# The opening of layer 0: vector order by hand, one loading queue, row weights through DRAM, three early pieces between first scores

## Chip, core and metric

The kernel runs on one core of one Trainium2 chip. The metric is device time in microseconds (us), the median of the runs shown. A separate profiled execution of the kernel gives the durations used for reasoning.

## The reference, cut to what matters

Four layers of attention and feed-forward run one after another on x of 4 batches (blocks) of 256 tokens by 256. The change lies in the attention of layer 0, which reads a context ctx of 1601 rows per block, and touches two later users of the context:

```python
# layer 0: attention of every token to its block's context
h = layernorm(x)                                   # 4 x 256 x 256
s = einsum('bsd,bmd->bsm', h, ctx) / 16            # 4 x 256 x 1601
s = where(mask[:, None, :], s, -1e30)
out = einsum('bsm,bmd->bsd', softmax(s), ctx)
x = x + where(any(mask, -1)[:, None, None], out, 0)
```

Layer 1 needs a weighted sum of the context rows. The weight of a row is a running sum of powers of sigmoid(decay), and a sum of these weights is needed too. Layer 2 needs keys and values of the context, products of ctx with weights, which depend on nothing that layers 0 and 1 compute.

## The kernel before, in words

Everything is fp32. Each program line is handed to a scheduler, which may reorder independent instructions of an engine; `pin` (line 99) holds an instruction behind the one that was written before it on the same engine. Each engine then works through its own list in order, and so do the queues on which SP and ACT issue DMAs.

`setup` (line 140) issues the loads of the four token blocks on SP's queue (L152) and lets POOL make the identity and constants.

`l0_xattn` (line 165) loads, for each block, the transposed context (ctxT; block 0 in four pieces, L183, the others whole, L136) and the plain context (ctxn, L188), on SP's queue. Two buffers hold ctxn, so the third load waits for a free one. Then it creates the generator of the early pieces (L190), which loads its weights (L1203, L1207). `hidden` (L192) brings a block's mask to all partitions by ACT's queue and turns it into an additive mask in two POOL steps. A second small mask load, and VectorE's muf, anym and anyd (L207 to L211), give for each block whether any row is valid; a product with ones spreads this to anyb. The row weights are a sigmoid on ACT (L216), a scan on one partition (L220) and a sum (L224). `spread_weights` (L230) copies them to all partitions by five products with a row of ones (L236) and five ACT copies (L238).

The main loop runs over 4 blocks and two halves q of 128 tokens. `turned` (L241) normalizes a block (statistics, root on ACT, reciprocal, scaling), turns it by four TensorE transposes (L248) and copies it (L250). `scores` (L253) makes the score products of one half (16 matmul instructions of up to 512 columns), adds the mask with a running maximum on VectorE (L260, two instructions), and takes the exponential on ACT (L268). Its PSUM tile has one buffer of four banks, so the next scores wait for this exponential. `values` (L274) turns the probabilities in groups of four (L284), evicts them alternately by VectorE and ACT (L71, L73) and multiplies with ctxn; the result goes into x (L297). The values of one half are written after the scores of the next. Last in each turn stands the weighted context sum csum for layer 1 (L314, eight in all), which needs ctxT and the spread weights.

An early piece (`l2_early`, line 1194) is either a product piece of layer 2's keys and values (8 matmul instructions, two ACT evictions, one store of va) or a turn piece (four transposes, one eviction, one store). There are 165: per unit seven product pieces, then four turns of the unit before. `fill(n)` (line 109) takes the next n of them. Fixed numbers are taken at fixed places: in `l0_ffn` 34 (F0, line 46), in `l0_add` 81 (G0), later 48, and the last two are taken in layer 2's attention, where the softmax of its first unit is prepared. Before the change none is taken in `l0_xattn`.

Of the kernel before, what the change touches and what calls it, by code (L numbers as in the profile page):

```python
# [11 lines left out]
F32 = mybir.dt.float32  # L12
BF16 = mybir.dt.bfloat16
U8 = mybir.dt.uint8
# [18 lines left out]
NEG = -1e30  # L33
# [7 lines left out]
NH2, NKV2, HD2 = 16, 4, 128  # L41
# [17 lines left out]
class Kernel:  # L59
    def __init__(self, ctx, tc, ins, out):  # L60
        self.ctx, self.tc, self.nc = ctx, tc, tc.nc
        self.i, self.out = ins, out
        self.flip = 0
        self.flip4 = False


# [73 lines left out]
    def setup(self):  # L140
        nc, tc, ctx, i = self.nc, self.tc, self.ctx, self.i
        const = self.const = ctx.enter_context(tc.tile_pool(name="const", bufs=1))
        self.small = ctx.enter_context(tc.tile_pool(name="small", bufs=3))
        xp = ctx.enter_context(tc.tile_pool(name="x", bufs=1))
        self.xn = ctx.enter_context(tc.tile_pool(name="xn", bufs=2))
        self.xnT = ctx.enter_context(tc.tile_pool(name="xnT", bufs=2))
        self.dram = ctx.enter_context(tc.tile_pool(name="dram", bufs=2, space=DRAM))

        self.x = []
        for b in range(B):  # L150
            t = xp.tile([P, 2, D], F32, name=f"x{b}")
            nc.sync.dma_start(t, i["x"][b].rearrange("(q p) d -> p q d", p=P))  # L152
            self.x.append(t)

        self.ident = const.tile([P, P], F32, name="ident")
        make_identity(nc, self.ident)
        self.ones = const.tile([P, P], F32, name="ones")
        nc.gpsimd.memset(self.ones, 1.0)
        self.eps5 = const.tile([P, 1], F32, name="eps5")
        nc.gpsimd.memset(self.eps5, 1e-5)  # L160
        self.eps6 = const.tile([P, 1], F32, name="eps6")
        nc.gpsimd.memset(self.eps6, 1e-6)


    def l0_xattn(self):
        nc, tc, i = self.nc, self.tc, self.i
        with ExitStack() as es:
            one = es.enter_context(tc.tile_pool(name="a0one", bufs=1))
            two = es.enter_context(tc.tile_pool(name="a0", bufs=2))
            ps_s = es.enter_context(tc.tile_pool(name="a0s", bufs=1, space=PSUM))  # L170
            ps = es.enter_context(tc.tile_pool(name="a0p", bufs=2, space=PSUM))
# [4 lines left out]
            ctxn, ctxT = [], []  # L176
            for b in range(B):
                pool = self.e2 if b < 2 else one
                if b == 0:
                    t = pool.tile([P, 2, MP], F32, name="ctxT", bufs=2)  # L180
                    v = i["ctxT"][b].rearrange("(k p) m -> p k m", p=P)
                    for c0 in range(0, MP, 512):
                        nc.sync.dma_start(t[:, :, c0 : min(MP, c0 + 512)], v[:, :, c0 : min(MP, c0 + 512)])  # L183
                else:
                    t = self.load_ctxT(pool, b, 2)
                ctxT.append(t)
                t = two.tile([P, NM, D], F32, name="ctxn")
                nc.sync.dma_start(t, i["ctx"][b].rearrange("(m p) d -> p m d", p=P))  # L188
                ctxn.append(t)
            self.early = self.l2_early(ctxT)  # L190

            def hidden(b):  # L192


                mu = two.tile([P, M], U8, name="mub")
                nc.scalar.dma_start(mu, i["mask"][b : b + 1].to_broadcast([P, M]))
                mf = two.tile([P, M], F32, name="mfb")
                nc.gpsimd.tensor_copy(mf, mu)
                nc.gpsimd.tensor_scalar(mf, mf, -NEG * 16.0, NEG * 16.0, ALU.mult, ALU.add)
                return mf  # L200
# [5 lines left out]
            muf = one.tile([B, M], F32, name="muf", tag="row")  # L206
            nc.vector.tensor_copy(muf, mu)  # L207
            anym = one.tile([B, 1], F32, name="anym")
            nc.vector.tensor_reduce(anym, muf, AX.X, ALU.max)
            anyd = one.tile([B, B], F32, name="anyd")  # L210
            nc.vector.tensor_scalar(anyd, self.ident[:B, :B], anym, None, ALU.mult)  # L211


            dec = one.tile([1, 1], F32, name="dec")
            nc.scalar.dma_start(dec, i["decay"])
            nc.scalar.activation(dec, dec, AF.Sigmoid)  # L216
            orow = one.tile([1, M], F32, name="orow", tag="row")
            nc.gpsimd.memset(orow, 1.0)
            wrow = one.tile([1, M], F32, name="wrow")
            nc.vector.tensor_tensor_scan(  # L220
                wrow[:, ::-1], dec.to_broadcast([1, M]), orow, 0.0, ALU.mult, ALU.add
            )
            sw = one.tile([1, 1], F32, name="sw")
            nc.vector.tensor_reduce(sw, wrow, AX.X, ALU.add)  # L224
            misc = ps1.tile([P, 512], F32, name="misc1", tag="misc")
            self.mm(misc[:, 0:B], self.ones[:B, :], anyd, True, True)
            anyb = one.tile([P, B], F32, name="anyb")
            nc.vector.tensor_copy(anyb, misc[:, 0:B])

            def spread_weights():  # L230
                w = one.tile([P, M], F32, name="wall")
                for c0, c1 in (*CC, (M, M + 1)):
                    t = ps1.tile([P, 512], F32, name="misc2", tag="misc")
                    row, to = (sw, self.swb) if c0 == M else (wrow[:, c0:c1], w[:, c0:c1])
                    tc.keep_in_program_order(
                        nc.tensor.matmul(t[:, : c1 - c0], self.ones[:1, :], row, start=True, stop=True)  # L236
                    )
                    nc.scalar.copy(to, t[:, : c1 - c0])  # L238
                return w
# [13 lines left out]
            def scores(b, q, xT):  # L253
                s = ps_s.tile([P, 2048], F32, name="s0")
                for c0, c1 in CC:
                    for k in range(2):
                        self.mm(s[:, c0:c1], xT[:, k, q * P : (q + 1) * P], ctxT[b][:, k, c0:c1], k == 0, k == 1)
# [10 lines left out]
                nc.scalar.activation(p, s[:, :M], AF.Exp, bias=nm, scale=1.0 / 16.0, accum_out=sm)  # L268
# [30 lines left out]
            last = wall = None  # L299
            xT = turned(0)  # L300
            for b in range(B):
                for q in range(2):
                    now = (b, q, *scores(b, q, xT))
                    if q == 1 and b + 1 < B:
                        xT = turned(b + 1)
                    if q == 0 and b + 1 < B:
                        mask.append(hidden(b + 1))
                    if last is not None:
                        values(*last)
                    if wall is None:  # L310
                        wall = spread_weights()

                    junk = one.tile([P, M], F32, name="junk0", tag="row")
                    nc.vector.tensor_tensor_reduce(  # L314
                        junk, ctxT[b][:, q, :M], wall, 1.0, 0.0, ALU.mult, ALU.add, self.csum[:, q, b : b + 1]
                    )
                    last = now
            values(*last)

# [874 lines left out]
    def l2_early(self, ctxT):  # L1194
# [9 lines left out]
        w = []  # L1204
# [7 lines left out]
        def products(u):  # L1212
# [3 lines left out]
            for m in range(0, NM, 2):  # L1216
# [3 lines left out]
                for t in range(n):  # L1220
                    for k in range(2):
                        c0 = (m + t) * P
                        self.mm(tp[:rows, t, :], ctxT[u // NKV2][:, k, c0 : c0 + rows], w[u % NKV2][:, k, :], k == 0, k == 1)
# [1016 lines left out]
```

## Time and profile before

| what | value |
|---|---|
| median of 3 runs | 2660.19 us (2654.16 to 2660.89) |
| the profiled execution's own time | 2609.97 us |
| its span, first to last instruction | 2608.2 us |
| mean granted TensorE clock | 0.979 |
| TensorE busy (matmuls) | 2472.6 us, 95% |
| VectorE, ScalarE (ACT), GpSimd (POOL) busy | 57%, 50%, 29% |
| first score product starts | 16.27 us |
| fourth scores (block 1, second half) start | 64.79 us |

A share is an average over the whole span; what a step of the opening costs has to be read from that stretch. In timeline lines the columns are start, duration (both us), engine, line, operation, output and inputs, count, and in brackets how long the engine stood idle before it and what ended that. The profiled execution is about 50 us shorter than the runs of the median, so differences within it are carried over, not its level.

### The profile page before, as it was taken

To read this page: it belongs to the slowest core of one execution; us is meant where nothing else is said; L and a number is where in the kernel's file an instruction comes from. 1 tells how busy PE (TensorE), PEld (TensorE's weight loads), DVE (VectorE), ACT (ScalarE), POOL (GpSimd) and SP (SyncE) were. 2 spreads that over 40 slices of the span, in tenths; PEclk is the share of its full clock that TensorE was granted. 3 is DMA by queue.
4 is the path that set the end of the run, shared out by engine and by line. 5 is a ranking of instruction groups with operands and counts; after the bars stand their busy time and mean duration, and the time that the engine had idled before them with its cause. 6 is when DMAs were issued, how large, how long until landed. Compare 5 with 4: busy or idle time off the path is not lost. (4 is left out here: it accounts for less than half of the span.)

```text
span 2608.2 us, 47024 instructions
## 1 busy us (share of the span) xinstructions
PE 2472.6 (95%) x17800; PEld 1512.2 (58%) x17816; DVE 1473.9 (57%) x3039; ACT 1307.1 (50%) x2955; POOL 751.9 (29%) x1030
## 2 busy tenths in 40 slices
PE   7989978999899999999999999998998999999997
PEld 4678967777455555555555555655564544545553
DVE  6344537635677777777777777673334314334323
ACT  2335545424544445444544454532326766857775
POOL 1015646132444334334334444332102001011000
PEclk8999999899999999999999999998999999999998
DMA  5155686626311111111111110004211100000000
GB/s 203 61 190 164 187 174 206 202 67 211 114 47 39 47 47 47 47 42 36 46 46 39 47 47 21 9 1 165 99 60 55 34 1 28 4 4 2 6 6 5
DMA packets 94654, 186.24 MB, mean 71 GB/s; under 512 B 15052, under 2 KB 62864, under 8 KB 93232
## 3 DMA queue, kind: packets, MB, share of 16 engines
q1 hardware_dynamic: 78278, 144.90, 16.4%
q0 software_dynamic: 10416, 28.46, 4.9%
q10 hardware_dynamic: 5738, 9.87, 1.2%
q8 instruction: 145, 2.38, 0.4%
q14 instruction: 77, 0.63, 0.1%
HBM read 136.77 MB, written 46.42 MB: 70 GB/s over the span
## 5 line engine op out<-in xcount | busy, mean ns | idle before, releaser
L1496 ACT ACTIVATE p<-s,nm 128x448 f32<-128x448 f32 (+1 forms) x512 | 326.9, 645 | 423.4 <-DVE nm L1492 259.1
L1957 ACT ACTIVATE e<-s 128x1024 f32<-128x1024 f32 (+1 forms) x448 | 404.3, 960 | 158.2 <-PE s L76 153.1
L76 PE MATMUL s<-kT,qT 128*32 128x448 f32 (+1 forms) x4096 | 470.2, 556 | 10.0 <-ACT p L1496 5.0
L76 PE MATMUL o<-pT,va 128*128 128x256 f32 (+2 forms) x1920 | 431.0, 376 | 6.1 <-DVE pT L1538 6.1
L1532 POOL TENSOR_SCALAR p<-p,rm 128x448 f32<-128x448 f32 (+1 forms) x512 | 323.3, 659 | 369.5 <-DVE rm L1525 339.2
L76 PEld LDWEIGHTS o<-pT,va 128*128 128x128 f32 (+1 forms) x1920 | 344.4, 191 | 93.0 <-issue 51.5
L1538 DVE STREAM_TRANSPOSE pT<-p 128x896 f32<-128x896 f32 (+1 forms) x256 | 283.8, 1127 | 37.2 <-POOL p L1532 33.5
L1492 DVE TENSOR_REDUCE nm<-s 128x2 f32<-128x896 f32 (+1 forms) x256 | 282.6, 1104 | 3.3
L76 PE MATMUL s<-qb,kT 32*128 32x256 f32 (+1 forms) x3328 | 267.6, 404 | 13.2 <-ACT e L1957 11.0
L76 PEld LDWEIGHTS s<-kT,qT 128*32 128x32 f32 x4096 | 123.6, 109 | 265.0 <-issue 223.4
L76 PE MATMUL o<-e,va 128*32 128x256 f32 (+1 forms) x3328 | 235.7, 391 | 1.2 <-DVE os L2054 1.2
L76 PEld LDWEIGHTS s<-qb,kT 32*128 32x128 f32 (+1 forms) x3328 | 162.9, 181 | 105.0 <-issue 75.4
L76 PEld LDWEIGHTS o<-e,va 128*32 128x32 f32 (+1 forms) x3328 | 90.5, 110 | 115.0 <-issue 74.9
L1984 POOL TENSOR_TENSOR x<-x,t 128x32 f32<-128x32 f32 x64 | 14.7, 252 | 438.4 <-DVE t L1979 438.4
L76 PE MATMUL fill<-wkc_early,ctxT 128*128 128x256 f32 (+1 forms) x532 | 130.7, 394 | 8.2 <-ACT kT_early L1252 7.8
L1489 DVE TENSOR_TENSOR s<-s,mask 128x128 f32<-128x128 f32 (+1 forms) x256 | 83.0, 325 | 67.5 <-PE s L76 62.8
L76 PEld LDWEIGHTS fill<-wkc_early,ctxT 128*128 128x128 f32 (+1 forms) x532 | 102.0, 196 | 26.2 <-ACT kT_early L1252 10.3
L431 POOL DMA_INDIRECT f0xr<-f0xd,f0src x95 | 92.0, 968 | 50.8 <-PE f0tph L488 42.3
L1384 POOL TENSOR_TENSOR qo<-qo,qt 128x512 f32<-128x512 f32 x32 | 41.1, 1284 | 225.2 <-DVE rm L1525 139.7
L1496 ACT ACTIVATION_READ_ACCUMULATOR p<-s,nm 128x1 f32 x512 | 101.7, 199 | 0.0
L76 PE MATMUL f2gu<-f2wgu,f2xsT 128*128 x176 | 85.6, 611 | 0.6 <-issue 0.3
L529 POOL DMA_INDIRECT f0yt<-f0yd,f0slot x64 | 66.8, 1044 | 47.5 <-DMA vd<-va_early 16.3
(517 smaller groups left out, 3567.4 us busy)
## 6 DMA issues: line engine op xcount, KB each, us to landing
ctxT<-in_ctxT SPq DMA_DIRECT2D x10, 1664.0 KB, 10.6
f0yd<-f0ys SPq DMA_DIRECT2D x95, 128.0 KB, 2.8
vd<-va_early SPq DMA_DIRECT2D x90, 128.0 KB, 2.5
kd<-kT_early SPq DMA_DIRECT2D x45, 256.0 KB, 2.5
kT<-kd SPq DMA_DIRECT2D x15, 768.0 KB, 4.2
va<-vd SPq DMA_DIRECT2D x15, 768.0 KB, 6.0
wq<-in_l_wq SPq DMA_DIRECT2D x16, 512.0 KB, 3.3
wo<-in_l_wo SPq DMA_DIRECT2D x16, 512.0 KB, 3.1
```

The lines of the kernel that those rows point to most:

```text
L76: self.nc.tensor.matmul(out, lhsT, rhs, start=start, stop=stop, **kw)
L431: nc.gpsimd.indirect_dma_start(out=t, out_offset=None, in_=xd[:, :], in_offset=bass.IndirectOffsetOnAxis(ap=src[:, n : n + 1], axis=0),)
L529: nc.gpsimd.indirect_dma_start(out=yt, out_offset=None, in_=yd[:, :], in_offset=bass.IndirectOffsetOnAxis(ap=slot[:, t, r : r + 1], axis=0),)
L1384: nc.gpsimd.tensor_tensor(o1, o1, t2, ALU.add)
L1489: nc.vector.tensor_tensor(sv, sv, mask[:, 2 * c : 2 * c + 2, : nt - CT, :].rearrange("p n t i -> p n (t i)"), ALU.add)
L1492: nc.vector.tensor_reduce(nm[:, 2 * c : 2 * c + 2], s[:, :, : nt * 32], AX.X, ALU.max, negate=True)
L1496: nc.scalar.activation(p[:, n, : nt * 32], s[:, n, : nt * 32], AF.Exp, bias=nm[:, e : e + 1], accum_out=sm[:, e : e + 1],)
L1532: nc.gpsimd.tensor_scalar(p[:, n, : nt * 32], p[:, n, : nt * 32], r[:, e : e + 1], 1.0, ALU.mult, ALU.mult)
L1538: nc.vector.transpose(pT[:, 2 * c : 2 * c + 2, :nt, :].rearrange("p n t i -> p n (t i)"), p[:, :, : nt * 32])
L1957: nc.scalar.activation(e[:kr, :, :n, :], s[t][:kr, :, :n, :], AF.Exp, scale=1.0 / math.sqrt(HD3))
L1984: nc.gpsimd.tensor_tensor(xt, xt, t[:, q], ALU.add)
```

## The change

- SP's queue gets the loads in the order: tokens of block 0, mask of block 0, ctxT of block 0, tokens of blocks 1 to 3, the early pieces' weights, then the other context loads as before. The masks of blocks 1 to 3 stay on ACT's queue, pinned.
- VectorE's work of the opening is pinned: the statistics and scaling of block 0, then the statistics of blocks 1 to 3, from which one root and one reciprocal serve three blocks. A dummy root loads ACT's table first; ten transposes of the identity with no use run on TensorE.
- The small mask load and muf, anym, anyd, anyb go. Whether any row is valid is read from the running maximum in the instruction that scales the result.
- The sigmoid becomes an exponential on ACT and an addition and reciprocal on VectorE. The scan follows the first mask addition; its sum is an accumulating ACT copy. The row goes to DRAM and comes back to all partitions by two DMAs on ACT's queue, in place of the five products and copies.
- The weighted sums of block 0 move into the first turn of block 1 (three in that turn), all pinned.
- After the first scores three early pieces are taken, their matmuls pinned on TensorE, as are the scores of block 0. `take` gives them tiles of the `tp` tag, which gets three buffers instead of two.

The diff, cut to its core:

```diff
-            nc.sync.dma_start(t, i["x"][b].rearrange("(q p) d -> p q d", p=P))
+        nc.scalar.activation(const.tile([P, 1], F32, name="root"), self.eps5, AF.Sqrt)
...
+            token(0)
+            nc.scalar.dma_start(dec, i["decay"])
+            hidden(0, nc.sync)
...
+                if b == 0:
+                    for n in range(1, B):
+                        token(n)
+                    self.early = self.l2_early(ctxT)
...
-            mu = one.tile([B, M], U8, name="mu")
-            nc.scalar.dma_start(mu, i["mask"])
-            mask = [hidden(0)]
-            nc.vector.tensor_copy(muf, mu)
-            nc.vector.tensor_reduce(anym, muf, AX.X, ALU.max)
-            nc.vector.tensor_scalar(anyd, self.ident[:B, :B], anym, None, ALU.mult)
-            nc.scalar.activation(dec, dec, AF.Sigmoid)
...
+            def weights():
+                self.pin(nc.vector.tensor_scalar(dec, dec, 1.0, None, ALU.add))
+                self.pin(nc.vector.reciprocal(dec, dec))
+                wrow = one.tile([1, M + 1], F32, name="wrow")
+                self.pin(nc.vector.tensor_tensor_scan(
+                    wrow[:, :M][:, ::-1], dec.to_broadcast([1, M]), self.ones[:1, :1].to_broadcast([1, M]), 0.0,
+                    ALU.mult, ALU.add,
+                ))
+                self.pin(nc.scalar.activation(junk, wrow[:, :M], AF.Copy, accum_out=wrow[:, M:]))
+                wd = self.dram.tile([1, M + 1], F32, name="wrowd")
+                nc.scalar.dma_start(wd, wrow)
+                nc.scalar.dma_start(wall, wd[:, :M].to_broadcast([P, M]))
+                nc.scalar.dma_start(self.swb, wd[:, M:].to_broadcast([P, 1]))
...
-                self.layernorm(xn, self.x[b])
+                for q in range(2):
+                    self.pin(nc.vector.tensor_scalar(
+                        xn[:, q, :], self.x[b][:, q, :], mv[:, b, q, 0:1], rs[:, b, q : q + 1], ALU.subtract, ALU.mult
+                    ))
...
+                        if b == 0:
+                            self.pin(ins)
...
+                if b + q == 0:
+                    weights()
...
-                nc.vector.tensor_tensor(r, r, anyb[:, b : b + 1], ALU.mult)
+                nc.vector.scalar_tensor_tensor(r, mx[:, 1:2], NEG * 8.0, r, ALU.is_gt, ALU.mult)
...
+            for n in range(10):
+                nc.tensor.transpose(t[:, :P], self.ident, self.ident)
...
+            for b0, b1 in ((0, 1), (1, B)):
+                for b in range(b0, b1):
+                    for q in range(2):
+                        st = self.small.tile([P, 6], F32, name="st0")
+                        self.pin(nc.vector.bn_stats(st, self.x[b][:, q, :]))
+                        self.pin(nc.vector.bn_aggr(mv[:, b, q, :], st))
+                self.rstd(rs[:, b0:b1], mv[:, b0:b1, :, 1], 1.0, self.eps5)
+                if b0 == 0:
+                    xT = turned(0)
+            self.pin(nc.scalar.activation(dec, dec, AF.Exp, scale=-1.0))
...
                     now = (b, q, *scores(b, q, xT))
+                    if last is None:
+                        self.hold = True
+                        self.fill(3)
+                        self.hold = False
...
+                    for c in [] if b == 0 else [(0, 0), (0, 1), (1, 0)] if (b, q) == (1, 0) else [(b, q)]:
+                        self.pin(nc.vector.tensor_tensor_reduce(
+                            junk, ctxT[c[0]][:, c[1], :M], wall, 1.0, 0.0, ALU.mult, ALU.add,
+                            self.csum[:, c[1], c[0] : c[0] + 1],
+                        ))
```

More of the change, by code (lines that the diff above doesn't have):

```diff
@@ L150, in setup @@
         for b in range(B):
[L151 to L153 removed]
+            self.x.append(xp.tile([P, 2, D], F32, name=f"x{b}"))
         self.ident = const.tile([P, P], F32, name="ident")
@@ L170, in l0_xattn, with token, hidden @@
             ps_s = es.enter_context(tc.tile_pool(name="a0s", bufs=1, space=PSUM))
-            ps = es.enter_context(tc.tile_pool(name="a0p", bufs=2, space=PSUM))
+            ps = es.enter_context(tc.tile_pool(name="a0p", bufs=3, space=PSUM))
             ps1 = es.enter_context(tc.tile_pool(name="a0q", bufs=1, space=PSUM))
             CC = [(c, min(M, c + 512)) for c in range(0, M, 512)]
-            ctxn, ctxT = [], []
+            ctxn, ctxT, mask = [], [], []
+            def token(b):
+                nc.sync.dma_start(self.x[b], i["x"][b].rearrange("(q p) d -> p q d", p=P))
+            def hidden(b, eng):
+                mu = two.tile([P, M], U8, name="mub")
+                ins = eng.dma_start(mu, i["mask"][b : b + 1].to_broadcast([P, M]))
+                if b:
+                    self.pin(ins)
+                mf = two.tile([P, M], F32, name="mfb")
+                nc.gpsimd.tensor_copy(mf, mu)
+                nc.gpsimd.tensor_scalar(mf, mf, -NEG * 16.0, NEG * 16.0, ALU.mult, ALU.add)
+                mask.append(mf)
+            dec = one.tile([1, 1], F32, name="dec")
+            token(0)
+            nc.scalar.dma_start(dec, i["decay"])
+            hidden(0, nc.sync)
             for b in range(B):
@@ L189, in l0_xattn @@
                 ctxn.append(t)
[L190 to L200, printed above, removed]
-            mu = one.tile([B, M], U8, name="mu")
@@ L204, in l0_xattn @@
-            nc.scalar.dma_start(mu, i["mask"])
-            mask = [hidden(0)]
-            muf = one.tile([B, M], F32, name="muf", tag="row")
-            nc.vector.tensor_copy(muf, mu)
-            anym = one.tile([B, 1], F32, name="anym")
-            nc.vector.tensor_reduce(anym, muf, AX.X, ALU.max)
[L210 to L215, printed above, removed]
@@ L216, in l0_xattn @@
-            nc.scalar.activation(dec, dec, AF.Sigmoid)
[L217 to L239, printed above, removed]
+            self.take = lambda: ps.tile([P, 512], F32, name="fill0", tag="tp")
@@ new lines, in l0_xattn @@
+            wall = one.tile([P, M], F32, name="wall")
+            def weights():
[6 more added lines that the diff above has]
+                ))
+                junk = one.tile([1, M], F32, name="junkw", tag="row")
+                self.pin(nc.scalar.activation(junk, wrow[:, :M], AF.Copy, accum_out=wrow[:, M:]))
[3 more added lines that the diff above has]
+                nc.scalar.dma_start(self.swb, wd[:, M:].to_broadcast([P, 1]))
@@ L256, in scores @@
                     for k in range(2):
-                        self.mm(s[:, c0:c1], xT[:, k, q * P : (q + 1) * P], ctxT[b][:, k, c0:c1], k == 0, k == 1)
+                        ins = nc.tensor.matmul(
+                            s[:, c0:c1], xT[:, k, q * P : (q + 1) * P], ctxT[b][:, k, c0:c1], start=k == 0, stop=k == 1
+                        )
+                        if b == 0:
+                            self.pin(ins)
                 mx = self.small.tile([P, 2], F32, name="mx0")
@@ L297, in values @@
                 nc.vector.scalar_tensor_tensor(xt, av, r, xt, ALU.mult, ALU.add)
-            last = wall = None
-            xT = turned(0)
+            t = ps.tile([P, 512], F32, name="idle", tag="tp")
+            for n in range(10):
+                nc.tensor.transpose(t[:, :P], self.ident, self.ident)
+            mv = one.tile([P, B, 2, 2], F32, name="mv0")
+            rs = one.tile([P, B, 2], F32, name="rs0")
+            for b0, b1 in ((0, 1), (1, B)):
[8 more added lines that the diff above has]
+            self.pin(nc.scalar.activation(dec, dec, AF.Exp, scale=-1.0))
+            last = None
             for b in range(B):
@@ L303, in l0_xattn @@
                     now = (b, q, *scores(b, q, xT))
+                    if last is None:
+                        self.hold = True
+                        self.fill(3)
+                        self.hold = False
                     if q == 1 and b + 1 < B:
@@ L306, in l0_xattn @@
                     if q == 0 and b + 1 < B:
-                        mask.append(hidden(b + 1))
+                        hidden(b + 1, nc.scalar)
                     if last is not None:
                         values(*last)
[L310 to L316, printed above, removed]
+                    for c in [] if b == 0 else [(0, 0), (0, 1), (1, 0)] if (b, q) == (1, 0) else [(b, q)]:
+                        junk = one.tile([P, M], F32, name="junk0", tag="row")
+                        self.pin(nc.vector.tensor_tensor_reduce(
+                            junk, ctxT[c[0]][:, c[1], :M], wall, 1.0, 0.0, ALU.mult, ALU.add,
+                            self.csum[:, c[1], c[0] : c[0] + 1],
+                        ))
                     last = now
@@ L1222, in products @@
                         c0 = (m + t) * P
-                        self.mm(tp[:rows, t, :], ctxT[u // NKV2][:, k, c0 : c0 + rows], w[u % NKV2][:, k, :], k == 0, k == 1)
+                        ins = nc.tensor.matmul(
+                            tp[:rows, t, :], ctxT[u // NKV2][:, k, c0 : c0 + rows], w[u % NKV2][:, k, :],
+                            start=k == 0, stop=k == 1,
+                        )
+                        if self.hold:
+                            self.pin(ins)
                 va = e2.tile([P, 2, HD2], F32, name="va_early", bufs=6)
```

## The prediction

> **What bounds the kernel now.** I read the page first: TensorE is busy 95% of the span, so nearly everything that delays it in one stage delays the end. The exceptions are the gather stages at 350 to 440 us, where the page's PE slices fall to 7 and 8 tenths. Then I cut the opening into stages (span:length, busy PE, PEld, DVE, ACT, POOL, clock, DMA share, GB/s):
>
> ```profile
> 0.00:16.27 16.27, 1.71 (x7) 1.18 (x7) 11.12 (x25) 4.54 (x8) 8.51 (x15) 1.00 0.83 273
> 16.27:40.30 24.03, 22.34 (x48) 9.49 (x49) 13.89 (x23) 5.58 (x9) 0.00 (x0) 0.79 1.00 365
> 40.30:64.80 24.50, 21.90 (x96) 16.35 (x95) 18.58 (x31) 6.35 (x9) 4.50 (x2) 0.93 0.01 1
> 64.80:92.30 27.50, 26.38 (x116) 18.41 (x115) 11.37 (x27) 8.52 (x12) 3.11 (x2) 1.00 0.23 72
> ```
>
> Until 16.27 us TensorE does 1.7 us of work. The second stage reads as full, but holds only two score products, which a settled stage does in 5.71 us each. The timeline says why:
>
> ```profile
> 3.67 0.43 DVE L90 BATCH_NORM_STATS2 ln_st<-x 128x6 f32<-128x256 f32 x1
> 8.49 0.29 ACT L80 ACTIVATE ln_rs<-ln_mv,eps 128x2 f32<-128x2 f32 x1
> 10.48 1.84 DVE L211 TENSOR_SCALAR anyd<-ident,anym 4x4 f32<-4x4 f32 x1
> 13.08 0.15 DVE L81 RECIPROCAL ln_rs<-ln_rs 128x2 f32<-128x2 f32 x1
> 14.84 3.45 DVE L220 TENSOR_TENSOR_SCAN wrow<-dec,orow 1x1601 f32<-1x1601 f32 x1
> 16.27 7.60 PE L76 MATMUL s<-ctxT,xT 128*128 128x512 f32 x16 [0.68 <-ACT xT L250]
> 26.75 0.59 ACT L238 COPY wall<-misc 128x512 f32<-128x512 f32 x1 [0.62 <-PE misc L236]
> 27.36 1.28 ACT L268 ACT_TABLE_LOAD   x1
> 28.65 1.60 ACT L268 ACTIVATE p<-s,nm 128x1601 f32<-128x1601 f32 x1
> 35.53 4.79 PE L76 MATMUL s<-ctxT,xT 128*128 128x512 f32 x12
> 57.27 5.41 PE L76 MATMUL av<-ctxn,pt 128*128 128x256 f32 x16 [1.25 <-DVE pt L71]
> ```
>
> The square root of token block 0 is out at 8.78; its reciprocal runs at 13.08, behind the statistics of other blocks and anyd. Later the exponential stands behind a wall copy and a table load, and the second scores are interleaved with row-weight products (L236) at half pace. At 57 us TensorE waits for an eviction which VectorE does late, because eight L314 sums fill it from 33 to 55 us. The same view, cut where the granted clock changes:
>
> ```profile
> 26.73:36.97 10.24, 8.65 (x12) 3.34 (x13) 4.05 (x6) 4.41 (x7) 0.00 (x0) 0.50 1.03 405
> 57.45:60.87 3.42, 3.42 (x9) 2.71 (x10) 1.49 (x6) 1.69 (x2) 0.00 (x0) 0.50 0.00 0
> ```
>
> Last, DMA over 0 to 60 us, in 40 slices of 1.5 us:
>
> ```profile
> GB/s 0 157 262 179 215 344 407 390 351 358 353 371 393 414 397 353 350 351 401 414 417 426 417 376 382 280 47 1 0 11 0 0 0 0 0 0 0 0 0 0
> ```
>
> Transfers run flat out till 39 us, so which of them is first matters.
>
> **What the Trainium skill says.** "TensorE: Matmul & The Clock Gate", What's actually happening: the clock is halved after an idle window of about 3.4 us and full after a busy one, the window running freely. The trace agrees: half-clock stretches of 10.24 and 3.42 us. The same page, Part 4, says transposes don't count as busy in the same way; no row here shows it. It makes me doubt that the ten idle transposes warm anything. "ScalarE: Activation LUTs", What ACT_TABLE_LOAD costs: about 1.28 us and a drain; the trace has 1.28. "DMA: Bandwidth & Descriptors", Issuing engines are not separate DMA queues: moving the mask from ACT's queue to SP's changes order, not bandwidth.
>
> **The change part by part.**
>
> 1. First tokens and VectorE's order. Block 0's first statistics start at 3.67 today, so x arrives by then; I keep that. Pinned: two halves of 0.64 (the pair at 79.41 to 80.05), to 5.0; hand-over and root 0.5, to 5.5 (its table is loaded earlier by the new dummy root); reciprocal 0.2; two xn of 0.41, to 6.5; four transposes, 1.12 as at 14.47, to 7.8; copy 0.59 and hand-overs, to 8.7. Scores start at 8.7 instead of 16.27. Have they data? In the new order 256 KB of x, 200 of mask and 512 of ctxT come first, 0.99 MB. The GB/s row sums to that at 6.4 us; with 2 us till the waiter sees it, 8.4. The second piece (1.51 MB) shows at 10.4, when it is needed (8.7 + 1.7). The mask's two POOL steps of 1.5 end by 9.
>
> 2. First scores. 7.60 today, of which 3.6 at half clock; 5.71 if warm. The idle transposes decide; I take 7.0: end at 15.7. Both ends: 14.4 and 16.3.
>
> 3. Between the scores. Mask addition 2.2, nm 0.15, exponential 1.8 and hand-overs make 4.7 us (today 23.87 to 30.39, with copy and table load). The three pieces are 24 matmuls at 1.75 per 8 (the row at 641.68 to 643.41): 5.2 us, pinned ahead of the second scores, so they set the pace, not the softmax. Their weights are 3.22 MB into the queue: 12.8 us, seen at 14.8, in time. The other blocks' statistics, pinned ahead of the mask addition, end at about 15.5 (x is 2.96 MB in: 12.1 + 2 + 1.3), under the cover of the scores. Weight products on TensorE and their copies go: they lie inside the 16.4 us from 23.87 to 40.3. Second scores end at 15.7 + 5.2 + 5.7 = 26.6, with 0.4 for hand-overs 27.0, against 40.3: **13.3 us earlier**.
>
> 4. Next values: 7.8 (40.3 to 48.1) plus 0.66 for the transposes of block 1, which now come here. Third scores at 35.5 against 48.10: 12.6 earlier. ctxn is 5.71 MB in: 19.8, seen at 21.8 and needed at 27. ctxT of block 1 (7.41 MB, more with wall and mask: 26) is needed at 35.5.
>
> 5. Third scores and values: 16.7 today (48.10 to 64.79); the next periods are 13.9, 13.6, 13.9. The L314 sums leave this stretch, and with them the late eviction and its half-clock window: minus 3.0. Fourth scores at 49.2 against 64.79: **15.6 earlier**.
>
> 6. What is given back. The sums (1.9 each with the accumulator read) now follow each x addition, beside 5.7 us of scores; three at once are 5.7 and delay a mask addition 0.5, unseen by TensorE. The last has no scores beside it: its values wait for VectorE's eviction, +1.3. Scan 3.45, add and reciprocal lie beside pieces and second scores. The DRAM trip: ACT waits for the row's landing before it can issue the broadcast; queued behind may be the second exponential and evictions. Not in the trace; nearest rows are stores of kr at 2.5 us and the slowest va store at 10.0. Issued about 24, needed for evictions at 28: bound 0 to 6; I take 1.0. A gain is excluded, as nothing waits for wall before 49. The masks of blocks 1 to 3 now go out one at a time on ACT's queue; the first at about 22, landing within 7 us (the slowest today), 3 us of POOL, ready at 32 and needed at 41. The three va stores join SP's queue behind the ctx loads; what follows them there waits for a free ctxn buffer anyway.
>
> 7. Pieces done early. They are 5.2 us less work later, but each later slot just runs three further pieces. At the end of layer 0's opening slots (34 pieces) pieces 35 to 37 are two products and a turn (4.1 us), so little is saved by then; the gather stages wait anyway; and the last slots drop three turns of 0.6 beside softmax preparation. Bounds: -2 (norms land elsewhere) to +5.2; I take 2.0.
>
> Sum: 15.6 + 2.0 - 1.3 - 1.0 = 15.3 us. The profiled execution took 2609.97 (span 2608.2): 2594.7. The median shown, 2660.19, is 50.2 above it; I carry the difference unchanged: **2644.9**, rounded to 2645.
>
> **Rivals.** (a) Larger: transposes do warm the clock and the pieces pay in full: 1.3 + 3.2 more, and no ACT wait, 1.0: gain 21, 2639. For: pieces are pure TensorE work and TensorE is 95% busy. Against: item 7.
> (b) Smaller: ACT is held on the DRAM row through evictions (6 instead of 1) with a cold window behind it (+1.7): gain 8.6, 2651.6. For: DMA share is 1.00 at that time. Against: the row is 6 KB.
> (c) Nothing: the freed time reappears in a later stage that doesn't start earlier, such as the gathers at 350 to 410 us (PE 28.9 of 40 busy). 2660. Against: their inputs come from the same chain, so they shift along; weight loads wait for the same buffers.
> (d) Slower: the pieces are pinned ahead of the second scores, and TensorE's stream can't pass them. If their weights land as today, behind all ctx loads (issue at 25.24, landing about 37), the second scores start at 43 and end near 49; 22 us later than in my sum: 15.3 - 22 = 7 slower, 2667. Break-even is a piece start at 31, and 0.3% is lost from about 39. Against: SP issues in the order written wherever no buffer is awaited, as its timeline shows.
>
> **How the numbers follow.** About 0.3%, 8 us, is what a measurement of this kernel can tell from no change. Forecast 0.62, (a) 0.17, (b) 0.10, (c) 0.05, (d) 0.06. The forecast's own range, from items 2, 6 and 7, is 2639 to 2651. The range reaches to (a) with a few us for shifted clock windows, and past (b): 2634 to 2655. Slower: (d). Same: (c) and half of (b), with a little of the forecast: 0.12. Faster 0.82.
>
> **What would show it.** After: first scores near 8.7 (item 1); pieces directly behind them and second scores at 21 (3); no half clock from 27 to 37 or at 57; fourth scores near 49 (5). Scores later than 12 mean data or VectorE's order fails me; a gap before the pieces means (d); an ACT wait before a DMA issue at 24 to 30 means (b); fourth scores at 49 with a total gain under 10 means item 7 or (c).

## The result, and the profile after

| | before | after |
|---|---|---|
| median | 2658.49 us (22 runs) | 2664.77 us (22 runs) |
| ratio after / before | | 1.0027, 95% interval 1.0018 to 1.0036 |
| profiled execution, its span | 2609.97, 2608.2 us | 2659.12, 2657.4 us |
| mean granted TensorE clock | 0.979 | 0.972 |
| first scores start / second scores end | 16.27 / 40.3 | 9.06 / 28.3 |
| third / fourth scores start | 48.10 / 64.79 | 44.31 / 57.78 |
| last scores (block 3, second half) start | 119.74 | 129.54 |

Slightly slower, where 15 us of gain were forecast. The sets of runs below were made on different chips, on which the kernel before takes 2658, 2622, 2619 or 2655 us; only ratios and differences within a set are used. (The two profiled executions of the table are 49 us apart for that reason, not through the change. Their openings can be compared: in a second profile of each kernel no score start moves by more than 1.3 us.)

(Behind the attention of layer 0 come its feed-forward stages: the router, which chooses experts for each token, the expert tiles, and the gathers, which fetch their results back per token.)

The table already has the shape of the answer. The opening runs ahead by 12.0 us at the end of the second scores, by 3.8 at the third, by 7.0 at the fourth, and is 9.8 behind at the last. Something is lost at each new block. The opening cut into stages at the same events as before (span:length, busy PE, PEld, DVE, ACT, POOL, clock, DMA share, GB/s): to the first scores, to the end of the second, to the fourth, and through block 1's second half and block 2's first.

```profile
0.00:9.06 9.06, 3.77 (x14) 2.68 (x15) 3.27 (x7) 2.37 (x4) 4.06 (x12) 1.00 0.64 205
9.06:28.50 19.44, 19.26 (x56) 11.07 (x56) 10.45 (x25) 7.64 (x14) 0.34 (x2) 1.00 1.08 369
28.50:57.80 29.30, 22.64 (x99) 17.23 (x100) 10.40 (x23) 6.94 (x10) 3.98 (x3) 0.88 0.49 177
57.80:94.70 36.90, 28.69 (x115) 20.27 (x114) 18.07 (x35) 8.52 (x12) 4.41 (x3) 0.86 0.18 52
```

The first two rows are as intended: TensorE starts at 9 us and is busy for 19.26 of 19.44. The last two are not: 6.7 and 8.2 us idle, at clocks of 0.88 and 0.86. No engine is near full in them, so it is a wait. The waits of TensorE up to 150 us (line, waited for: us in total, times, longest), in the kernel after and then in the one before, name it:

```profile
PE tp_ln L246 <- DVE xn L240: 23.6, 6, 7.8
```

```profile
PE tp_ln L248 <- DVE xn L94: 1.5, 1, 1.5
```

The four transposes of a block wait for its scaling xn; before, only those of block 0 did. The timeline of the kernel after, with the lines that answer to those of before:

```profile
3.69 0.43 DVE L316 BATCH_NORM_STATS2 st<-x 128x6 f32<-128x256 f32 x1 [3.69 <-DMA x<-in_x]
5.22 0.17 DVE L82 RECIPROCAL rs<-rs 128x2 f32<-128x2 f32 x1 [0.36 <-ACT rs L81]
9.06 8.49 PE L255 MATMUL s<-ctxT,xT 128*128 128x512 f32 x16 [0.68 <-ACT xT L248]
17.38 5.40 PE L1249 MATMUL fill<-wkc_early,ctxT 128*128 128x256 f32 x24
22.62 5.71 PE L255 MATMUL s<-ctxT,xT 128*128 128x512 f32 x16
33.78 0.45 PE L246 MATMUL tp_ln<-ident,xn 128*128 128x128 f32 x1 [5.45 <-DVE xn L240]
```

The reciprocal runs at 5.22 instead of 13.08, 1.1 us after the first statistics end; the pieces follow the first scores without a gap, and the second scores follow them. From 28.3 on TensorE waits. The transfers of the opening are as dense as before and end some 2 us later. And here is the whole machine at block 2, where the same thing costs 7.81 us:

```profile
57.78 5.71 PE L255 MATMUL s<-ctxT,xT 128*128 128x512 f32 x16
...
67.54 1.28 ACT L272 ACT_TABLE_LOAD   x1 [3.86 <-DVE nm L267]
68.84 1.60 ACT L272 ACTIVATE p<-s,nm 128x1601 f32<-128x1601 f32 x1
...
70.56 0.16 DVE L275 RECIPROCAL r<-sm 128x1 f32<-128x1 f32 x1 [3.11 <-ACT p L272]
70.75 0.16 DVE L276 SCALAR_TENSOR_TENSOR r<-mx,r 128x1 f32<-128x1 f32 x1
70.83 0.73 DVE L240 TENSOR_SCALAR xn<-x,mv,rs 128x256 f32<-128x256 f32 x2
71.29 1.23 PE L246 MATMUL tp_ln<-ident,xn 128*128 128x128 f32 x4 [7.81 <-DVE xn L240]
72.31 1.91 PE L289 MATMUL tp<-ident,p 128*128 128x128 f32 x8
```

Read it from below. The turns of the values (L289) use probabilities of the half before, whose exponential ran at 53.43 to 55.03; they could have begun when the scores ended at 63.48. They stand behind the block's transposes (L246) in TensorE's list, and these wait for xn. Nothing in xn's data is late: its mean and root were there at 16 us. But L240 is pinned, so it stays behind the instruction written before it on VectorE, the scaled reciprocal L276, and that needs the sum of the exponential of the scores just made. So the block's preparation, once free filling for VectorE, now ends the chain scores, mask addition, exponential, reciprocal, and TensorE waits out the whole softmax with ready work behind it.

With each of these gaps goes a stretch at half clock. The same stage view of the kernel after, cut at those stretches:

```profile
31.60:38.40 6.80, 3.64 (x14) 2.95 (x15) 2.87 (x5) 2.45 (x4) 3.15 (x2) 0.50 1.02 416
65.70:75.90 10.20, 4.61 (x16) 3.87 (x17) 3.35 (x11) 4.14 (x5) 0.00 (x0) 0.50 0.00 0
103.20:110.10 6.90, 3.37 (x13) 2.90 (x14) 3.04 (x9) 3.68 (x5) 0.00 (x0) 0.51 0.17 59
```

They hold 11.6 us of TensorE work at half pace, about 5.8 us lost (an estimate: half of that work's time). With the waits of blocks 1 to 3 (23.6 less 3.1 at block 0) that is 26, less what TensorE would have waited there for other things.

### The profile page after: what moved, and what is told of

Read it like the earlier page. It is cut to its first block, busy times and chain, and to the rows that moved or that the text cites. A ratio compares the mean times of both kernels' runs of the same rounds, so it can differ in the third digit from the quotient of the medians.

```text
span 2657.4 us, 47023 instructions
## 1 busy us (share of the span) xinstructions
PE 2490.8 (94%) x17798; PEld 1521.0 (57%) x17814; DVE 1461.7 (55%) x3026; ACT 1303.1 (49%) x2951; POOL 755.9 (28%) x1037
## 5 line engine op out<-in xcount | busy, mean ns | idle before, releaser
L1988 ACT ACTIVATE e<-s 128x1024 f32<-128x1024 f32 (+1 forms) x448 | 404.4, 960 | 159.5 <-PE s L77 154.7
L2015 POOL TENSOR_TENSOR x<-x,t 128x32 f32<-128x32 f32 x64 | 14.7, 252 | 439.8 <-DVE t L2010 439.8
L77 PE MATMUL f0gu<-f0w,f0xsT 128*128 x380 | 79.5, 332 | 1.8 <-DMA vd<-va_early 1.1
```

Source lines behind the costliest of these rows:

```text
L77: self.nc.tensor.matmul(out, lhsT, rhs, start=start, stop=stop, **kw)
L1988: nc.scalar.activation(e[:kr, :, :n, :], s[t][:kr, :, :n, :], AF.Exp, scale=1.0 / math.sqrt(HD3))
L2015: nc.gpsimd.tensor_tensor(xt, xt, t[:, q], ALU.add)
```

## The experiments

Two theories went in. **One:** the pin on L240, with the transposes written ahead of the values, makes the loss, and the rest of the change works as forecast. **Two:** the loss comes from the traffic and the order of queues (the row through DRAM, masks and weights on new queues), and xn is late only because all of that is.

### The kernel before, once more

No edit.

> The kernel before, unchanged, for a second profile: the first one was 50 us shorter than its runs, and that of the changed kernel only 7. Theory one (the opening alone decides): the opening is as in the first profile (fourth scores near 64.8 us, first router product near 141.8), and the span is near 2655 because stages behind 210 us are longer, the expert tiles of layer 0 taking about 160 us instead of 144.7. Theory two (the change lengthens the expert tiles and what follows): the expert tiles take about 145 us again.

Measured: 2617.52 us beside a median of 2621.81; scores at 16.30, 30.73, 48.59, 65.28, and the last at 120.23. Of theory one, the opening came and the span did not: the expert tiles take 144.9 us again, as theory two has it. But the runs beside it, on this chip, are as short, so the level may be one of the chip; this run can't tell, and the kernel after is measured once more below. The opening is a property of the kernel.

### The scaling of blocks 1 to 3 left free

```diff
-                    self.pin(nc.vector.tensor_scalar(
+                    ins = nc.vector.tensor_scalar(
...
+                    if b == 0:
+                        self.pin(ins)
```

> The changed kernel with one edit: the scaling of blocks 1 to 3 is no longer pinned on VectorE, so it stands before the first mask addition (blocks 1 and 2) or in the first turn (block 3). Theory one: the 23.6 us that TensorE waits for xn ahead of its block transposes go, and with them three half-clock windows; the starts of the third, fifth and seventh scores come 7 to 10 us earlier each, 22 to 26 us together, and the median is near 2641. Theory two (the loss lies in the pieces taken early or in later stages): the waits go but the end comes less than 8 us earlier, above 2655.

Measured: 2597.88 against 2621.81 us, ratio 0.992 (0.9894 to 0.9947). One edit turns the small loss into a gain of 24 us. Scores start at 8.45, 21.60, 36.33 and 49.79, the last at 105.06. The waits of TensorE from 12 to 150 us in this kernel have no xn left, and from 11.3 us on the clock is full:

```profile
PE f0gu L77 <- issue: 2.2, 1, 2.2
PE av L77 <- DVE pt L72: 2.1, 4, 1.1
PE tp L291 <- ACT pt L74: 1.4, 5, 0.3
```

```profile
11.30:185.40 174.10, 163.02 (x761) 122.01 (x760) 95.82 (x249) 62.14 (x117) 23.30 (x26) 1.00 0.52 173
```

TensorE is busy 163 of 174 us. From second to third scores it is 14.73 us instead of 21.69, at block 2 14.88 instead of 23.50, at block 3 13.46 instead of 21.34: 23.5 us in three steps of 7.0, 8.6 and 7.9. Theory two is out: queues, DRAM trip and pieces are unchanged here (ACT's queue issues the store of the row, block 1's mask and the broadcast at 25.27, 25.56 and 30.23; at 25.55, 25.86 and 30.29 in the change as made).

### The scaling left pinned, the transposes put behind the values

```diff
-                        xT = turned(b + 1)
+                        xn = turned(b + 1)
...
                         values(*last)
+                    if q == 1 and b + 1 < B:
+                        xT = across(xn, True)
```

(across holds the transposes and the copy, the transposes pinned.)

> The changed kernel with the scaling pinned as it is, but the transposes of the next block pinned on TensorE behind the values instead of ahead of them. Theory one in its full form (it takes both the late scaling and a TensorE list in which the transposes stand ahead of the values): TensorE no longer waits for xn ahead of the values; about 1.5 us per block is paid for transposes and copy right before the scores, so the time falls by 14 to 21 us against the changed kernel, to 2644 to 2651. If the late scaling alone were to blame, whatever TensorE's order: near 2665.

Measured: 2595.54 us, ratio 0.9912 (0.9886 to 0.9939), last scores at 103.12. TensorE's timeline of this kernel, with block 1's scaling on VectorE:

```profile
31.91 1.41 DVE L281 SCALAR_TENSOR_TENSOR r<-mx,r 128x1 f32<-128x1 f32 x1
...
33.24 0.72 DVE L240 TENSOR_SCALAR xn<-x,mv,rs 128x256 f32<-128x256 f32 x2
34.45 0.60 PE L249 MATMUL tp_ln<-ident,xn 128*128 128x128 f32 x4
```

xn is as late as in the kernel after (33.2), behind the same reciprocal, and nobody waits: the values fill TensorE until 34.45. So a late xn alone costs nothing that can be seen here, nor does the order of the transposes alone (in the run before they stand ahead of the values and xn is early). It takes both.

The Trainium skill bears on this: "TensorE: Matmul & The Clock Gate", Step-by-step: what each phase is for, says that matmuls stay in program order and that only weight loads are pulled ahead. The trace agrees: values ready since 55 us stood 7.81 us behind a waiting transpose.

### The kernel before with that pin alone

```diff
-                self.layernorm(xn, self.x[b])
+                for q in range(2):
+                    ins = nc.vector.tensor_scalar(
+                        xn[:, q, :], self.x[b][:, q, :], mv[:, b, q, 0:1], rs[:, b, q : q + 1], ALU.subtract, ALU.mult
+                    )
+                    if b:
+                        self.pin(ins)
```

(with the statistics of all blocks made up front, not pinned.)

> The kernel before with only this part of the change: statistics of all blocks up front and free as they were, the scaling of blocks 1 to 3 pinned behind what was written before it on VectorE, the reciprocal row sum that needs the exponential. Theory one: TensorE waits before the transposes of blocks 1, 2 and 3, some 5 to 8 us each with a half-clock window behind, and the time rises by 18 to 28 us, to 2677 to 2687. Theory two: within 5 us of the kernel before.

Measured: 2653.86 against 2621.81 us, ratio 1.0134 (1.0103 to 1.0164), 32 us, more than the 18 to 28 expected. The waits up to 150 us have the line of the kernel after, and the timeline shows why the longest is 12.07: here the sums for layer 1 (L327) fill VectorE ahead of the pinned scaling.

```profile
PE tp_ln L253 <- DVE xn L245: 26.3, 4, 12.1
```

```profile
49.81 2.98 POOL L199 TENSOR_SCALAR mfb<-mfb 128x1601 f32<-128x1601 f32 x1
...
51.45 3.02 DVE L327 CUSTOM_DVE_ANT_0 junk<-ctxT,wall 128x1601 f32<-128x1601 f32 x1
...
54.39 0.15 DVE L276 TENSOR_TENSOR r<-r,anyb 128x1 f32<-128x1 f32 x1
54.46 0.73 DVE L245 TENSOR_SCALAR xn<-x,mv,rs 128x256 f32<-128x256 f32 x2
54.92 1.22 PE L253 MATMUL tp_ln<-ident,xn 128*128 128x128 f32 x4 [12.07 <-DVE xn L245]
```

The pin, with the statistics that it needs up front (not tested by themselves), makes the loss; no queue, DRAM trip or piece of the change is in this kernel.

### The kernel after, once more

No edit.

> The changed kernel, unchanged, beside the kernel before on the same chip, since levels of chips differ by some 40 us. Theory one: the ratio to the kernel before is again 1.000 to 1.006, TensorE waits 22 to 25 us for xn ahead of the block transposes, the last scores start about 10 us later than before, and the stages behind 210 us take as long as before on this chip, within 5 us. Theory two (later stages are lengthened by the change): the expert tiles of layer 0 take over 10 us longer than in the kernel before.

Measured: 2623.88 (20 runs) against 2619.01 us (31 runs), ratio 1.0019 (1.001 to 1.0028). xn is waited for 22.5 us. The last scores start 10.3 us later than in the second profile of before (of another chip, at a level 0.1% away), the first product of the router 11.1 later, but the last exponential of layer 3 only 5.5: some 5 us come back after the opening. The expert tiles of layer 0 take 148.4 us, 3.5 more than in that profile and not the 10 of theory two; in the first profile of this same kernel, on its slower chip, they took 159.5. So that lengthening goes with the chip, as far as these profiles tell.

### Without the three pieces

The fill(3) of the version with the free scaling is taken out.

> The changed kernel with free scaling of blocks 1 to 3 and without the three early pieces between the first scores (they are taken later, as before). If the pieces pay what the prediction took (2 us, at most 5): the second scores start about as early, since the softmax needs 4.7 us in any case, the clock may fall for a window there, and the time is 1 to 5 us above that of the version with free scaling, ratio to before near 0.993 to 0.995. If the pieces cost (their norms collide with the router): faster than the version with free scaling by more than 2 us.

Measured: 2600.41 against 2619.01 us, ratio 0.9936 (0.991 to 0.9961); with the pieces it was 0.992 of another set. TensorE's timeline of this kernel, and the stage view of what follows:

```profile
22.18 8.45 PE L257 MATMUL s<-ctxT,xT 128*128 128x512 f32 x16 [4.41 <-ACT p L274]
```

```profile
20.70:27.50 6.80, 5.32 (x7) 2.21 (x8) 3.67 (x3) 3.06 (x4) 0.86 (x1) 0.50 1.04 381
```

Without them TensorE idles 4.41 us between the scores, and the second scores run at half clock (8.45 instead of 5.81): the last scores start 2.0 us later than with the pieces, of which 0.6 were there when the second scores began. The expert tiles end 2.2 us earlier than with the pieces; up to layer 2's first queries (641 us) the lead over before stays at 16.5 us, where that of the version with pieces grows from 14.2 to 23.3. By these two traces the pieces would be worth 7 us, but they are no fair pair: the profiled execution with the pieces is the shortest of its four runs (2594.46, median 2597.88), this one the longest (2604.24, median 2600.41). By the ratios it is 4 (0.0016 of 2620), and their intervals overlap. So what the pieces are worth at the end isn't shown; the gap that they fill, and the half clock behind it, are.

### TensorE warmed with products in place of transposes

```diff
-            for n in range(10):
-                nc.tensor.transpose(t[:, :P], self.ident, self.ident)
+            for n in range(3):
+                nc.tensor.matmul(
+                    t.rearrange("p (n e) -> p n e", n=4), self.ident,
+                    self.ident[:, None, :].to_broadcast([P, 4, P]), start=True, stop=True,
+                )
```

(on the version with the free scaling; like the transposes, these products feed nothing.)

> The changed kernel with free scaling and with three 512-column products of the identity in place of the ten idle transposes; they add nothing to the output. If transposes don't count for TensorE's clock and products do: the clock is full by about 8 us, the first scores take 5.7 to 6.5 us instead of 7.2, bounded then by ctxT, and the end comes 1 to 2 us earlier, which the times can hardly show but the trace can. If either warms as well or as badly: first scores 7 us or more.

Measured: 2597.28 against 2619.01 us, ratio 0.9928 (0.9903 to 0.9952), no gain over 0.992. The weight loads of the first scores tell the clock, one a matmul; first the kernel after, then this one:

```profile
13.49 0.33 PEld L255 LDWEIGHTS s<-ctxT,xT 128*128 128x128 f32 x1 [0.52 <-issue]
14.34 0.26 PEld L255 LDWEIGHTS s<-ctxT,xT 128*128 128x128 f32 x1 [0.52 <-issue]
14.85 0.19 PEld L255 LDWEIGHTS s<-ctxT,xT 128*128 128x128 f32 x1 [0.24 <-DMA wkc_early<-in_l_wkc]
15.28 0.19 PEld L255 LDWEIGHTS s<-ctxT,xT 128*128 128x128 f32 x1 [0.24 <-issue]
```

```profile
9.10 0.19 PEld L257 LDWEIGHTS s<-ctxT,xT 128*128 128x128 f32 x1 [0.24 <-issue]
9.53 0.19 PEld L257 LDWEIGHTS s<-ctxT,xT 128*128 128x128 f32 x1 [0.24 <-issue]
...
14.67 5.45 PE L1254 MATMUL fill<-wkc_early,ctxT 128*128 128x256 f32 x24 [0.30 <-DMA wkc_early<-in_l_wkc]
21.75 1.55 PE L257 MATMUL s<-ctxT,xT 128*128 128x512 f32 x3 [1.63 <-ACT p L274]
```

0.85 us from one to the next is half the pace of 0.43; it ends at 14.5 in the kernel after. (The clock column of the stage views reads 1.00 here all the same, so in the opening I go by the pace.) With products the step is 0.43 from the start and the first scores take 5.78. The second scores come no earlier (21.75), because they wait for the exponential, and the first mask addition (17.59) stands on VectorE behind the other blocks' statistics, which end at 15.7 us, and their scalings.

### The kernel before with the sums moved

Only the three-in-one-turn order of the sums for layer 1, and their pins, are taken over.

> The kernel before with only the weighted context sums moved as in the change (none in block 0's turns, three in the first of block 1, all pinned). Item 5 of the prediction: the eviction behind the sums is no longer late, the half-clock window near 57 us goes, the fourth scores start 2.5 to 3.5 us earlier, at about 62, and the rest follows; about 1 us is given back at the last values. Against it: the third period stays at 16.7 us and the time is that of the kernel before within 1 us.

Measured: 2615.61 (12 runs) against 2619.01 us, ratio 0.999 (0.9979 to 1.0001). The stretch around the late eviction, from 44 to 66 us, in this kernel and then in the one before:

```profile
44.00:66.00 22.00, 21.33 (x87) 14.69 (x86) 9.19 (x21) 5.76 (x8) 2.58 (x2) 1.00 0.11 36
```

```profile
44.00:66.00 22.00, 20.07 (x79) 14.30 (x78) 15.88 (x27) 5.39 (x8) 3.56 (x2) 0.92 0.00 1
```

VectorE has 6.7 us less to do and the half-clock window is gone; the fourth scores start at 62.14 instead of 65.28. At the last scores 1.9 of these 3.1 us are left: the period with the three sums, from the fourth to the fifth scores, takes 15.17 us instead of 13.90. The medians are 3.4 apart, and the interval of the ratio just includes no change.

### Products for warming, the transposes behind the values

This joins the edits of two runs above.

> The version with the block transposes behind the values, and three products of the identity in place of the idle transposes. With free scaling the products made the first scores 1.4 us shorter, but the second scores started no earlier, for the first mask addition waited for the other blocks' statistics. If that is the bound, the same here: first scores 5.8 us, second scores near 21, time as that of the version without (ratio to before 0.990 to 0.993).

Measured: 2638.13 against 2655.47 us, ratio 0.9931 (0.9911 to 0.9951). First scores in 5.81 us, mask addition at 16.14, second scores at 20.31, last at 104.01; no gain over 0.9912 that the intervals can tell. The bound named in the expectation is tried next.

### And the statistics of the other blocks behind the first mask addition

```diff
-            for b0, b1 in ((0, 1), (1, B)):
+            def measured(b0, b1):
...
+                        measured(1, B)
```

(called for blocks 1 to 3 after the first scan.)

> As the one before, with the statistics of blocks 1 to 3 (pinned) moved behind the first mask addition and the row-weight scan. If these statistics held the first mask addition, it now starts right after the first scores, near 14.6 us instead of 17, and the second scores start where the three pieces end, near 20 instead of 21: 1 to 1.5 us earlier. ACT loads two more tables (1.28 us each), under the second scores. Ratio to before 0.989 to 0.992; if ACT's tables delay the second exponential, no gain.

Measured: 2640.88 against 2655.47 us, ratio 0.9939 (0.9917 to 0.996). The near end came as expected: mask addition at 14.47, second scores at 19.68. But the fourth scores start at 51.62 instead of 48.62. The timeline of this kernel:

```profile
26.60 0.36 ACTq L233 DMA_DIRECT2D wall<-wrowd  x1
...
27.48 0.44 ACTq L186 DMA_DIRECT2D mub<-in_mask  x1
41.64 1.52 POOL L190 CAST mfb<-mub 128x1601 f32<-128x1601 uint8 x1 [31.75 <-DMA mub<-in_mask]
...
44.82 1.23 DVE L267 CUSTOM_DVE_ANT_0 s<-s,mfb 128x1024 f32<-128x1024 f32 x1 [9.35 <-POOL mfb L191]
```

Block 1's mask now goes out behind the 800 KB of the row's broadcast; without this edit it went out at 24.28, ahead of the broadcast at 28.65, and POOL could start at 31.92. The third mask addition waited for it. VectorE's order was improved, and ACT's queue, whose program lines are the same, came out in another order.

### A shorter later slot

On the version with the transposes behind the values, the last of layer 0's opening slots takes one piece instead of four, so that the three early ones are left out there.

```diff
-F0 = [0, 0, 0, 0, 6, 8, 4, 4]
+F0 = [0, 0, 0, 0, 6, 8, 4, 1]
```

> The version with the block transposes behind the values, with three pieces fewer in the last slot ahead of layer 0's expert tiles (4 becomes 1), so that from there on all slots hold the same pieces as in the kernel before. If the three early pieces pay only where as many are left out: the expert tiles start 3 to 5 us earlier than without the edit, and the lead over the kernel before then stays constant through the gathers (374 to 610 us), where the unedited version's lead grows by 9. If the gather stages gain by something else: the lead grows there as well.

Measured: 2637.14 against 2655.47 us, ratio 0.9924 (0.9902 to 0.9947). Its neighbour in the set (the one with products; third scores within 0.2 us) starts the gathers at 372.7, this one at 365.5. They end at 480.3 and 479.1, and layer 2's first queries come at 676.0 and 678.6. The 7.2 us are gone within the gathers. (No trace of the kernel before at this chip's level exists, so the lead over it, of which the expectation spoke, can't be read; against the neighbour it isn't constant.) The ratios don't tell this version from 0.9931 or 0.9912: that it matters where the three pieces are left out isn't shown.

## Why the prediction was wrong

**The step that failed is the fourth**, "Next values: 7.8 (40.3 to 48.1) plus 0.66 for the transposes of block 1, which now come here. Third scores at 35.5". It priced the transposes by their own duration and asked neither when their input is made nor what stands behind them. From the end of the second scores to the start of the third it reckoned with 7.8 + 0.66 = 8.5 us; measured are 16.0 (28.33 to 44.31), and 8.9 (27.41 to 36.33) where only the pin is lifted. In between lie the waits of 5.45 and 0.98 us for xn and about 1.8 lost of the 3.64 us of work at half clock: 8.2, less 1.1 that TensorE waits in that stage without the pin. The same wait then comes at blocks 2 and 3 (7.81 and 6.29), to which the prediction carried the gain unchanged. The diff had it in plain sight: a pinned scaling written right after scores, whose last VectorE instruction needs the exponential. In the kernel before xn of blocks 1 to 3 ran between 18 and 27 us, in VectorE's idle time, so no profile of before could show a wait, and I took a step without a wait for one that can't get one:

```profile
18.21 0.38 DVE L94 TENSOR_SCALAR xn<-x,ln_mv,ln_rs 128x256 f32<-128x256 f32 x1
...
20.25 0.39 DVE L94 TENSOR_SCALAR xn<-x,ln_mv,ln_rs 128x256 f32<-128x256 f32 x1
...
24.85 0.66 PE L248 MATMUL tp_ln<-ident,xn 128*128 128x128 f32 x4
```

**Item by item**, from the version in which only that pin is lifted. First scores: 8.7 forecast, 8.45 (9.06 in the change as made); the 8.45 is set by the landing of ctxT, put at 8.4, the 9.06 by block 0's scaling, which took 2.00 us beside POOL's mask step where 0.8 was taken. They lasted 7.19 and 8.49, 7.0 forecast; the second is outside the bounds of 5.7 to 7.6, since its clock came full only at 14.5. End of the second scores: 27.0 forecast, 27.4 and 28.3. Third scores: 35.5, and 36.33. Third period: 13.7, and 13.46 (in the change as made 13.47). Fourth scores: 49.2, and 49.79; 15.0 or 15.5 ahead of the two profiles of before where 15.6 were forecast. The run with the sums moved confirms the 3.0 of that item as 3.1. Item 3's claim that the pieces and not the softmax set the pace holds in the change as made, and by 0.7 us not in the version with the free scaling.

**What is given back.** From the last scores to the router's first product it is 22.84 us instead of 22.07: 0.8 for the last sum, 1.3 forecast. But item 6 had the three sums in one turn "unseen by TensorE", and they are seen: in the version with the free scaling the fourth scores' mask addition stands behind them until 57.06, 1.6 us after these scores end, and the period to the fifth scores is 14.88 us where the same period a block later is 13.46. So 1.4 us more are given back, as in the run with the sums moved. The DRAM trip has 4.7 us between the store's issue and the broadcast's, ACT standing in between, as rival (b) had it. But in the change as made it delayed the second exponential by only 0.3 (row maximum out at 30.76, exponential at 31.23, of which 0.2 is a hand-over), and the evictions there came later anyway: 1.0 forecast.

**The pieces:** 2.0 forecast (bounds -2 to 5.2); 4 by the ratios, with intervals that leave nothing as well as 10 open. What I left out is that they also fill a gap behind which the clock is otherwise at half (up to 2.0 at the last scores).

**The rivals.** None had the mechanism. (a) with 2639, 21 us of gain, is near what the change gives without the pin (0.992; its interval of 14 to 28 us holds the forecast's 15.3 too), but that is luck: the transposes, which (a) needed to warm, don't. (d), the slower one, needed the weights to land at 31 us or later; they were there at 14.7 (the pieces' start with products for warming). The slower mechanism was of its kind, TensorE's stream pinned behind something late, in another place. In the change as made it costs 23.5 us up to the last scores and 26 at the end (1.0019 less 0.992, of 2620, from two sets, so within some 7 us), against a gain of some 21 to 24 by the rest: within these bounds that is the whole result.

**Open:** what the pieces are worth at the end, and what in the gathers takes back a lead of 7 us that reaches them. The version with the transposes behind the values has the lowest ratio, 0.9912 of before, but the intervals don't tell it from the other versions without the wait.

## What to carry to other kernels

A pin is an edge: for every pinned instruction ask what the one before it waits for, and for everyone who reads its result ask what ready work stands behind the reader. Late work on one engine is free until an in-order neighbour has something else queued behind the use of it; moving the use behind that ready work mends it as well as moving the work forward. And an edit to one engine's order can reorder another's DMA queue.

## What the runs showed of the hardware

- **Ten transposes left the clock at half, three products had it full.** With ten fp32 transposes ahead (2.40 us) the first scores began at half pace in all six profiles and took 7.19 to 8.49 us; with three products of 512 columns (4.4 to 5.5 us from the same start) they ran at full pace in all three and took 5.78 to 5.81. "TensorE: Matmul & The Clock Gate", Part 4, says that transposes don't count as busy in the same way; the runs agree with that, but the products also ran longer, so kind and length of the work aren't told apart.
- **A row by way of DRAM took 4 to 5 us.** In the version with the free scaling the store was issued at 25.27, the broadcast that reads it at 30.23, and ACT stood still for the landing; in three others it was 4.3 to 4.7:

```profile
30.23 0.35 ACTq L233 DMA_DIRECT2D wall<-wrowd  x1
...
31.10 0.59 ACT L250 COPY xT<-tp_ln 128x512 f32<-128x512 f32 x1 [4.36 <-DMA wrowd<-wrow]
```

- **VectorE's sum and POOL's mask step take turns.** The sum of 1601 columns takes 1.82 us alone, but 3.02 beside POOL's mask step, which itself takes 2.98 instead of 1.53 (the lines of the kernel before with the pin). The lengths fit waiting, not sharing: the sum that starts at 51.45 would end at 54.61 if it ran its 1.82 after POOL's step ends (52.79), and it ends at 54.47. "SBUF — State Buffer", Who interferes with whom, has it that a VectorE instruction with two SBUF inputs contends with a POOL instruction that reads SBUF; the trace agrees.
